# Router stage of a graph network: a buffer for every tile of neighbour rows, gates of edge-free nodes by place, a fixed order on PE

## The chip, the cores and the metric

The kernel runs on one core of one Trainium2 chip. Its time is the device time in microseconds (us) of one execution; with one core there is no other to wait for. The core has separate engines that run side by side, each with its own queue of instructions: PE (TensorE, matmuls; PEld is its weight loads), DVE (VectorE), ACT (ScalarE), POOL (GpSimd) and SP (SyncE, which here only starts transfers). They wait for each other through semaphores. [...] an *indirect* transfer takes one row of a table for each of the 128 partitions, by a column of indices, and here POOL starts all of these.

## The reference

A graph network of two layers over 3125 nodes with 256 features. The change concerns the last part, a mixture of four experts whose router looks at a node's neighbours. Cut to what matters:

```python
def _forward(x, edge_index, W_gat, att_src, att_dst, b_gat, ln_gamma, ln_beta, W1, b1, W2, b2):
    h = (x_flat @ W_gat).reshape(M, HEADS, NUM_EXPERTS)          # 4 heads x 4 experts
    loops = jnp.arange(M)                                         # every node is its own neighbour too
    src = concatenate([edge_index[0], loops]); dst = concatenate([edge_index[1], loops])
    e = leaky_relu((h * att_src).sum(-1)[src] + (h * att_dst).sum(-1)[dst], 0.2)
    ee = exp(e - segment_max(e, dst)[dst])
    alpha = ee / (segment_sum(ee, dst)[dst] + 1e-16)
    agg = segment_sum(h[src] * alpha[:, :, None], dst).reshape(M, 16) + b_gat
    scores = _layernorm(agg, ln_gamma, ln_beta).reshape(M, HEADS, NUM_EXPERTS).mean(1)
    topk_s, topk_i = top_k(scores, 2)
    w = softmax(topk_s, axis=-1)
    for ei in range(NUM_EXPERTS):
        g = where(topk_i == ei, w, 0.0).sum(-1)
        hh = gelu(x @ W1[ei] + b1[ei])
        out = out + g[..., None] * (hh @ W2[ei] + b2[ei])
```

A node without incoming edges has only itself as a neighbour, so its `alpha` is 1 and its `agg` is its own `h` plus the bias.

## The kernel before

The nodes lie in 25 tiles of 128 (`NT`). The layers before the router keep them in one order ("places"); the result rows `xs` of that order stay in SBUF. For the router's attention the nodes are sorted anew by their number of edges: in this second order 16 tiles are *busy* and need 36, 23, 21, ... 10 neighbour slots (`SLOTS2`, 279 in all), and 9 tiles are *free*, without edges.

The layer code has a helper `router_rows` that is called in six parts. For up to five tiles it normalizes the rows, stores them transposed to DRAM (`normed`, on SP), makes `h` (16 values) and the source attention (4 values) per node as `hx`, and scatters these 20 values by node number into a DRAM table `htab` (on POOL).

`routed_by_slots` is the router stage. It starts at about 2536 us and runs to the end.

- **Gathers.** L2107 fetches the 20 values of each node of the second order from `htab`, 25 gathers, free tiles first. `neighbours(t)` (L2137) fetches one row per neighbour slot into a tile `ed` with one gather for every slot (L2140). The tiles `ed` share three buffers: `more(3)` starts three tiles' gathers before the main loop, and `more(1)` the next after each `attend`.
- **Attention and gates.** `attend` (L2145) adds the two attention terms, takes leaky relu and maximum on DVE, the exp on ACT (L2156), and sums up the weighted rows on DVE (L2158). `gates` (L2168) takes up to five tiles: bias, layernorm (sqrt on ACT, L2194), mean over heads, the two best of four, their softmax (exp on ACT, L2215). At its end it makes, tile by tile, a 0/1 matrix `los` on DVE (L2228, three buffers) and a matmul (L2229) that adds the gates into a PSUM tile `placed` at the nodes' places. `own` (L2161) stands in for `attend` for the free tiles. `step` (L2244) does one busy tile, or five free ones, as a whole: it writes DVE, ACT and PE work in one go.
- **Experts.** The main loop takes four tiles at a time (the last time one), loads their transposed rows `xT` (L2330), and for each pair of experts calls `hidden` twice and later `outs`. `hidden` (L2261): 16 matmuls into four PSUM tiles `ph` (L2267, three buffers) and four gelus on ACT (L2269). `outs` (L2272): for each tile a bias matmul (L2276) and 8 matmuls (L2279) into a PSUM tile `po` (three buffers). Each float32 matmul is two passes on PE, and so two records in the profile. The outputs of the first 20 tiles (`NF`) are copied to `f` in SBUF by ACT (L2282), since the gates are not known yet. From the 21st tile on, all steps that are left are run, `gate` is copied out of `placed` (L2287), and the outputs are added to `xs` straight from PSUM (`add`, L2298).
- **Kept tiles.** With each tile of the last five, two of the 20 kept tiles are finished too, once for each pair of experts: `kept` does four `add`s from `f` on DVE. `put` scatters a finished tile to the output (L2303, POOL).
- **Order.** For ACT and DVE the program order is the order on the engine (`manual_schedule`). PE, POOL and SP are ordered by a scheduler. The main loop keeps a `clock`, 2.4 us per tile for a `hidden` and 4.6 us per tile for a pair of `outs`; before each `hidden` it runs the steps whose estimated gather time (1.25 us a slot) plus 8 lies before that clock.

Of the kernel before, what the change touches and what calls it, by code (L numbers as in the profile page):

```python
# [12 lines left out]
F32 = mybir.dt.float32  # L13
BF16 = mybir.dt.bfloat16
I32 = mybir.dt.int32
AF = mybir.ActivationFunctionType
# [5 lines left out]
P = 128  # L22
N = 3125
D = 256
# [872 lines left out]
class Fast(Net):  # L897
# [955 lines left out]
    def layers(self):  # L1853
# [7 lines left out]
        with ExitStack() as octx:  # L1861
# [40 lines left out]
            with tc.tile_pool(name="l1_edge", bufs=2, reuse_waits="tile") as ep, \  # L1902
# [93 lines left out]

                def router_rows(ts):
# [12 lines left out]
                    for i, t in enumerate(ts):  # L2010
# [11 lines left out]
                                            axis=AX.X, op=OP.add)  # L2022
                    for i, t in enumerate(ts):
                        ins = nc.gpsimd.indirect_dma_start(
                            out=self.htab[:NP, :], in_=hx[:, i, :], in_offset=None,
                            out_offset=bass.IndirectOffsetOnAxis(ap=self.pid[:, t:t + 1], axis=0)).ins

                        if t:
                            tc.declare_no_dep(ins, group="htab", reason="other nodes")
                        tc.add_to_no_dep_group("htab", ins)  # L2030
# [59 lines left out]
    def routed_by_slots(self):  # L2090
# [6 lines left out]
        free = [t for t in range(NT) if not SLOTS2[t]]  # L2097
        busy = [t for t in range(NT) if SLOTS2[t]]
        with ExitStack() as ctx:
# [4 lines left out]
                engines={mybir.EngineType.Activation, mybir.EngineType.DVE}))  # L2104
            hx = keep.tile([P, NT, 24], F32, name="hx")
            for t in free + busy:
                nc.gpsimd.indirect_dma_start(  # L2107
                    out=hx[:, t, :20], out_offset=None, in_=self.htab[:, :],
                    in_offset=bass.IndirectOffsetOnAxis(ap=self.pid2[:, t:t + 1], axis=0))
# [12 lines left out]
            for j, n in enumerate(("gat_asrc", "gat_adst", "gat_b", "gat_gamma", "gat_beta")):  # L2122
# [4 lines left out]
            his = keep.tile([P, NT, NT], F32, name="his")  # L2127
            nc.vector.tensor_tensor(his, self.iota[:, None, :NT].to_broadcast([P, NT, NT]),
                                    self.place2[:, 0].unsqueeze(2).to_broadcast([P, NT, NT]), op=OP.is_equal)
            placed = ps.tile([P, NT, NE], F32, name="placed")  # L2130
            f = keep.tile([P, NF, NE, D], F32, name="f")
# [4 lines left out]
            def neighbours(t):  # L2136
                S = SLOTS2[t]  # L2137
                ed = work.tile([P, max(SLOTS2) + 1, 20], F32, name="ed", bufs=3)
                for s in range(S):
                    nc.gpsimd.indirect_dma_start(  # L2140
                        out=ed[:, s, :], out_offset=None, in_=self.htab[:, :],
                        in_offset=bass.IndirectOffsetOnAxis(ap=self.nbrs[t][:, s:s + 1], axis=0))
                return ed

            def attend(t, ed, agg):  # L2145
# [9 lines left out]
                nc.vector.tensor_sub(e, e, m.to_broadcast([P, S + 1, 4]))  # L2155
                nc.scalar.activation(e, e, AF.Exp)  # L2156
# [4 lines left out]
            def own(ts):  # L2161

                agg = work.tile([P, 5, 20], F32, name="agg")
                nc.vector.tensor_copy(agg[:, :len(ts), :16], hx[:, ts[0]:ts[-1] + 1, :16])
                nc.vector.memset(agg[:, :, 16:], 1.0)
                return agg

            def gates(ts, agg):  # L2168

                n = len(ts)  # L2170
                t0 = ts[0]
# [11 lines left out]
                s = work.tile([P, 5, 8], F32, name="s")[:, :n]  # L2183
# [7 lines left out]
                tmp = work.tile([P, 5, 16], F32, name="tmp")[:, :n]  # L2191
                nc.vector.tensor_mul(tmp, f16, f16)
                nc.vector.tensor_reduce(s[:, :, 1], tmp, axis=AX.X, op=OP.add)
                nc.scalar.activation(s[:, :, 2], s[:, :, 1], AF.Sqrt, bias=self.eps[:, 0:1], scale=1.0 / 16)  # L2194
# [4 lines left out]
                sco = work.tile([P, 5, NE], F32, name="sco")[:, :n]  # L2199
# [3 lines left out]
                pick = work.tile([P, 2, 5, NE], F32, name="pick")  # L2203
                for j in range(2):
# [7 lines left out]
                    if j == 0:  # L2212
                        nc.vector.scalar_tensor_tensor(sco, o, -BIG, sco, op0=OP.mult, op1=OP.add)
                nc.vector.tensor_sub(s[:, :, 5], s[:, :, 5], s[:, :, 4])
                nc.scalar.activation(s[:, :, 5], s[:, :, 5], AF.Exp)  # L2215
# [5 lines left out]
                nc.vector.tensor_add(pick[:, 0, :n], pick[:, 0, :n], pick[:, 1, :n])  # L2221

                what = work.tile([P, 5, NT, NE], F32, name="what", bufs=1)
                nc.vector.tensor_mul(what[:, :n], his[:, t0:t0 + n].unsqueeze(3).to_broadcast([P, n, NT, NE]),
                                     pick[:, 0, :n].unsqueeze(2).to_broadcast([P, n, NT, NE]))
                for i, t in enumerate(ts):
                    los = work.tile([P, P], F32, name="los", bufs=3)
                    nc.vector.tensor_scalar(los, self.iota, self.place2[:, 1, t:t + 1], None, op0=OP.is_equal)  # L2228
                    nc.tensor.matmul(placed, los, what[:, i], start=(t == order[0]), stop=(t == order[-1]))  # L2229


            order = free + busy
            steps = []
            now = 1.25 * NT + 4
            for i in range(0, len(free), 5):
                steps.append((now, free[i:i + 5], None))
# [7 lines left out]
            def more(ahead):  # L2244

                for t in busy[len(eds):len(eds) + ahead]:
                    eds[t] = neighbours(t)

            def step():
                _, ts, t = steps.pop(0)  # L2250
                if t is None:
                    gates(ts, own(ts))
                    return
                if ts[0] not in aggs:
                    aggs[ts[0]] = work.tile([P, 5, 20], F32, name="agg")
                attend(t, eds[t], aggs[ts[0]][:, t - ts[0], :])
                more(1)
                if t == ts[-1]:
                    gates(ts, aggs[ts[0]])
# [12 lines left out]
            def outs(ts, hs, e0):  # L2272

                for j, t in enumerate(ts):
                    po = ps.tile([P, 2, D], F32, name="po", bufs=3)
# [8 lines left out]
                    if steps or len(done) == 0:  # L2284
                        while steps:
                            step()
                        nc.vector.tensor_copy(gate, placed)  # L2287
                        done.append(True)
# [4 lines left out]
                    for _ in range(2):  # L2293
                        if late:
                            kept(late.pop(0))
# [15 lines left out]
            def kept(t):  # L2311
                for e in range(NE):
                    add(t, e, f[:, t, e, :])
                put(t)

            done = []
            puts = []
            late = list(range(NF))

            tmp = work.tile([P, NT, 16], F32, name="what", bufs=1)  # L2320
            nc.vector.tensor_mul(tmp, hx[:, :, :16], att[:, 1:2, :].to_broadcast([P, NT, 16]))
            nc.vector.tensor_reduce(hx[:, :, 20:], tmp.rearrange("p t (h e) -> p t h e", e=4), axis=AX.X, op=OP.add)
            more(3)
            clock = 0.0
            last = None
            for t0 in range(0, NT, 4):
# [4 lines left out]
                for e0 in (0, 2):  # L2331
                    hs = []
                    for e in (e0, e0 + 1):
                        while steps and steps[0][0] + 8 < clock:
                            step()
                        hs.append(hidden(ts, xT, e))
                        clock += 2.4 * w
                        if e == e0 and last:
                            outs(*last)
                            last = None  # L2340
                    clock += 4.6 * w
                    last = ts, hs, e0
# [90 lines left out]
```

## Time and profile before

| | us |
|---|---|
| three runs | 3212.45, 3179.78, 3209.07 |
| their median | 3209.07 |
| the profiled execution | 3207.38 |
| its span | 3205.6 |
| busy in the span: PE | 1915.6 |
| PEld | 1173.4 |
| DVE | 1484.3 |
| ACT | 787.2 |
| POOL | 1580.0 |

The span runs from the first to the last instruction that the profiler recorded on this core. 1.8 us of the execution lie around it. The router's stretch, 2540 to 3206 us, has these rows (instruction group, partitions x elements, count, then busy us and mean ns of one, then idle time of the engine just before them and what ended it):

```profile
L2107 POOL DMA_INDIRECT hx<-htab,pid x25 | 23.7, 949 | 12.2 <-issue 7.3 <-DMA htab<-hx,pid 4.9
L2267 PE MATMUL ph<-xT,w 128*128 128x512 f32 x384 | 197.5, 664 | 64.7 <-ACT h L2269 38.3 <-issue 17.0 <-DMA xT<-normed 9.3
L2269 ACT ACTIVATE h<-ph,b 128x512 f32<-128x512 f32 x96 | 63.5, 687 | 215.6 <-PE ph L2267 116.9 <-remote 70.0 <-PE po L2279 15.0
L2282 ACT COPY f<-po 128x512 f32<-128x512 f32 x40 | 22.5, 588 | 210.9 <-remote 140.7 <-PE po L2279 66.0 <-PE po L2276 4.1
L2298 DVE SCALAR_TENSOR_TENSOR xs<-f,gate,xs 128x256 f32<-128x256 f32 x80 | 37.8, 483 | 2.1
L2303 POOL DMA_INDIRECT out<-xs,pid x25 | 25.1, 1003 | 56.7 <-DVE xs L2298 55.3 <-issue 1.5
```

"issue" means that the engine waited for nothing that the profile shows; "remote" that the releaser was not made out. The profile also gives the span in 40 equal slices of 80 us, with the busy share of each engine in tenths and the clock that TensorE was granted (`PEclk`, tenths of full speed), and can cut any stretch into windows with each engine's busy time and number of instructions.

### The profile page before, as it was taken

What the parts mean: (1) busy time and instruction counts of PE and PEld (TensorE: products, weight loads), DVE (VectorE), ACT (ScalarE), POOL (GpSimd) and SP (SyncE); (2) the same over time, 40 slices, a digit from 0 to 9 for tenths busy, and PEclk for the clock granted to TensorE, in tenths of its full rate; (3) what the DMA queues carried; (4) which work ended last, traced back from release to release, by engine and by line L of the source; (5) the groups of instructions that cost most, each with busy time, mean ns of one, the idle gap of its engine ahead of it and who ended that gap; (6) DMA issues with size and microseconds to landing.
All of it is one profiled execution on the core that took longest, in us unless ns stands there. A gap on an engine that the chain in (4) does not pass through costs nothing. (4 is left out here: it accounts for less than half of the span.)

```text
span 3205.6 us, 25047 instructions
## 1 busy us (share of the span) xinstructions
PE 1915.6 (60%) x7318; PEld 1173.4 (37%) x7318; DVE 1484.3 (46%) x4053; ACT 787.2 (25%) x2273; POOL 1580.0 (49%) x1675
## 2 busy tenths in 40 slices
PE   0166754567566768777726364755556534866678
PEld 0133432234333434443414243534334312533346
DVE  6366556544444545310436565866657301111027
ACT  1022221111111212111205242434344301322122
POOL 3555446746535453446165664546551272445443
PEclk9887876778778889888857676767666666978789
DMA  4522223222212221100064464546451200000001
GB/s 129 161 75 76 60 82 100 79 63 83 74 47 78 67 74 53 34 14 20 32 195 140 138 178 130 150 131 177 141 156 53 77 9 10 12 6 13 12 7 42
DMA packets 121376, 254.52 MB, mean 79 GB/s; under 512 B 36594, under 2 KB 61926, under 8 KB 120972
## 3 DMA queue, kind: packets, MB, share of 16 engines
q0 software_dynamic: 82656, 196.67, 21.7%
q1 hardware_dynamic: 31688, 49.09, 4.6%
q10 hardware_dynamic: 6884, 7.04, 0.7%
q8 instruction: 61, 1.00, 0.1%
q14 instruction: 87, 0.71, 0.1%
HBM read 228.93 MB, written 23.76 MB: 79 GB/s over the span
## 5 line engine op out<-in xcount | busy, mean ns | idle before, releaser
L1384 POOL DMA_INDIRECT g<-xtab,src x444 | 441.9, 995 | 413.4 <-DVE ed L1287 134.6
L1929 POOL DMA_INDIRECT kv<-kvtab,src x444 | 430.0, 968 | 317.4 <-issue 113.4
L2140 POOL DMA_INDIRECT ed<-htab,nb x279 | 264.7, 949 | 281.3 <-issue 184.0
L1966 ACT ACTIVATE kv<-kv,sc 128x64 f32<-128x64 f32 x1196 | 293.2, 334 | 52.9 <-issue 31.9
L1240 POOL DMA_INDIRECT gl<-gsrc,sidx x256 | 251.7, 983 | 79.1 <-issue 77.7
L1968 PE MATMUL pu<-kv,ident 128*128 128x256 f32 x888 | 270.1, 449 | 17.5 <-ACT kv L1966 12.1
L2279 PE MATMUL po<-w,h 128*128 128x256 f32 x800 | 210.5, 406 | 89.5 <-issue 88.8
L2267 PE MATMUL ph<-xT,w 128*128 128x512 f32 (+1 forms) x448 | 205.2, 609 | 64.7 <-ACT h L2269 38.3
L1706 PE MATMUL ph<-xT,w 128*128 128x512 f32 (+1 forms) x448 | 237.4, 660 | 0.0
L1723 PE MATMUL po<-w,h 128*128 128x256 f32 x800 | 218.0, 417 | 11.1 <-ACT h L1709 10.1
L1968 PEld LDWEIGHTS pu<-kv,ident 128*128 128x128 f32 x888 | 184.4, 223 | 67.2 <-ACT kv L1966 32.2
L1391 DVE SCALAR_TENSOR_TENSOR acc<-g,wt,acc 128x256 f32<-128x256 f32 x419 | 202.9, 484 | 12.2 <-DVE acc L1391 0.2
L2279 PEld LDWEIGHTS po<-w,h 128*128 128x128 f32 x800 | 156.8, 200 | 141.2 <-issue 123.6
L1935 DVE TENSOR_TENSOR kv<-kv,pr 128x1024 f32<-128x1024 f32 (+3 forms) x121 | 132.8, 1124 | 109.2 <-remote 70.4
L1723 PEld LDWEIGHTS po<-w,h 128*128 128x128 f32 x800 | 157.3, 207 | 48.6 <-issue 18.5
L1709 ACT ACTIVATE h<-ph,b 128x512 f32<-128x512 f32 (+1 forms) x112 | 71.7, 641 | 383.0 <-PE ph L1707 168.9
L1354 PE MATMUL pT<-typT,sel 18*128 18x128 bf16 (+9 forms) x229 | 32.9, 275 | 197.3 <-DVE typT L1345 145.1
L2267 PEld LDWEIGHTS ph<-xT,w 128*128 128x128 f32 x448 | 87.4, 210 | 165.8 <-issue 117.2
L1368 PE MATMUL pr<-self.relb,ohT 128*128 128x128 bf16 x687 | 82.7, 276 | 105.1 <-issue 57.6
L2158 DVE TENSOR_TENSOR ed<-ed 128x288 f32<-128x288 f32 (+12 forms) x16 | 7.5, 466 | 285.5 <-ACT ed L2156 285.5
L1756 POOL DMA_INDIRECT kvtab<-kv,pid x25 | 24.3, 972 | 224.6 <-DVE kv L1750 139.2
L1937 DVE TENSOR_TENSOR kv<-kv,q 128x1024 f32<-128x1024 f32 (+3 forms) x121 | 132.4, 1123 | 0.0
(443 smaller groups left out, 3197.3 us busy)
## 6 DMA issues: line engine op xcount, KB each, us to landing
dr<-in_gat_dst_row SPq DMA_DIRECT2D x32, 512.0 KB
g<-xtab,src POOLq DMA_INDIRECT x444
kv<-kvtab,src POOLq DMA_INDIRECT x444
own<-xq SPq DMA_DIRECT2D x25, 256.0 KB
xq<-own SPq DMA_DIRECT2D x25, 256.0 KB
ed<-htab,nb POOLq DMA_INDIRECT x279
w<-in_ex_w ACTq DMA_DIRECT2D x2, 2048.0 KB
gl<-gsrc,sidx POOLq DMA_INDIRECT x256
```

The costliest lines, as they stand in the source:

```text
L1240: ins = nc.gpsimd.indirect_dma_start(out=self.gl[:, :], out_offset=bass.IndirectOffsetOnAxis(ap=self.sidx2[:, c:c + 1], axis=0), in_=self. ...
L1384: self.moved = nc.gpsimd.indirect_dma_start(out=g[:, s % 4, :], out_offset=None, in_=self.xtab[:, :], in_offset=bass.IndirectOffsetOnAxis( ...
L1391: nc.vector.scalar_tensor_tensor(acc, g[:, s % 4, :], self.wts[t][:, s:s + 1], acc, op0=OP.mult, op1=OP.add)
L1706: nc.tensor.matmul(ph[:, :n], w1[:, k, mc], xT[:, k, :n], start=(k == 0), stop=False)
L1723: nc.tensor.matmul(pos[j // 2][:, j % 2], this[:, j * P:(j + 1) * P], w2[:, m, :], start=False, stop=(m == M - 1 and (j % 2 == 1 or j == w ...
L1929: nc.gpsimd.indirect_dma_start(out=kv[:, j, :], out_offset=None, in_=kvtab[:, :], in_offset=bass.IndirectOffsetOnAxis(ap=self.srcs[t][:, g ...
L1935: nc.vector.tensor_tensor(k4, k4, rr[:, r0:r0 + n].unsqueeze(2).to_broadcast([P, n, 4, HD]), op=OP.add)
L1966: nc.scalar.activation(v[:, h * HD:(h + 1) * HD], v[:, h * HD:(h + 1) * HD], AF.Copy, scale=sc[:, s, h:h + 1])
L1968: nc.tensor.matmul(pu, self.ident, v, start=(s == 0), stop=(s == SLOTS[t] - 1))
L2140: nc.gpsimd.indirect_dma_start(out=ed[:, s, :], out_offset=None, in_=self.htab[:, :], in_offset=bass.IndirectOffsetOnAxis(ap=self.nbrs[t][ ...
L2267: nc.tensor.matmul(ph[:, :w], w1[:, e, k, m * P:(m + 1) * P], xT[:, :len(ts), k, :], start=(k == 0), stop=(k == KB - 1))
L2279: nc.tensor.matmul(po[:, i], hs[i][:, m, j * P:(j + 1) * P], w2[:, e0 + i, m, :], start=False, stop=(i == 1 and m == M - 1))
```

## The change

1. `router_rows` also stores `hx` to a new DRAM tile `hown`, in the order of places (six stores on SP).
2. PE is added to `manual_schedule`: the program order is now PE's order too.
3. `hx` is gathered for the 16 busy tiles only. `ed` has a buffer of its own for every tile, and `neighbours` is called for all 16 tiles before the main loop.
4. Nodes without edges: `gates` is run once over all 25 tiles at the start of the stage, on `hown` (one load on SP), with the result in place order; it goes without `los` and `placed`. Once `placed` is complete, nodes whose sum of gates there is under 0.25 take the gates of this pass.
5. `attend`, `gates` and the new `to_places` are generators. They yield before an exp, a sqrt and the `placed` matmuls, and `go_on` takes every open one a stage further before each `hidden`.
6. `los` has four buffers instead of three, `po` four instead of three; `f` is allocated after the pass over 25 tiles, in its space.
7. `weighed`: eight of the 20 kept tiles are weighted on PE. For each expert ACT makes a diagonal matrix of the gates, and a matmul adds the weighted `f` into a PSUM tile; DVE adds that once.

```diff
...
+                self.hown = self.dram.tile([P, NT, 20], F32, name="hown")
...
                                             axis=AX.X, op=OP.add)
+                    nc.sync.dma_start(self.hown[:, t0:t0 + n, :], hx[:, :n, :])
...
-                engines={mybir.EngineType.Activation, mybir.EngineType.DVE}))
-            hx = keep.tile([P, NT, 24], F32, name="hx")
-            for t in free + busy:
+                engines={mybir.EngineType.Activation, mybir.EngineType.DVE, mybir.EngineType.PE}))
+            nb = len(busy)
+            hx = keep.tile([P, nb, 24], F32, name="hx")
+            for t in busy:
                 nc.gpsimd.indirect_dma_start(
...
-            f = keep.tile([P, NF, NE, D], F32, name="f")
...
-                ed = work.tile([P, max(SLOTS2) + 1, 20], F32, name="ed", bufs=3)
+                ed = keep.tile([P, S + 1, 20], F32, name=f"ed{t}")
...
+                yield
                 nc.scalar.activation(e, e, AF.Exp)
...
-            def own(ts):
-
-                agg = work.tile([P, 5, 20], F32, name="agg")
-                nc.vector.tensor_copy(agg[:, :len(ts), :16], hx[:, ts[0]:ts[-1] + 1, :16])
-                nc.vector.memset(agg[:, :, 16:], 1.0)
-                return agg
-
-            def gates(ts, agg):
-
-                n = len(ts)
-                t0 = ts[0]
+            def gates(n, agg, pool, most, out):
...
+                out.append(pick[:, 0, :n])
+
+            def to_places(ts, g):
+
+                n, t0 = len(ts), ts[0]
+                what = work.tile([P, 4, NT, NE], F32, name="what", bufs=1)
...
+                loss = []
+                for t in ts:
+                    loss.append(work.tile([P, P], F32, name="los", bufs=4))
+                    nc.vector.tensor_scalar(loss[-1], self.iota, self.place2[:, 1, t:t + 1], None, op0=OP.is_equal)
+                yield
                 for i, t in enumerate(ts):
-                    los = work.tile([P, P], F32, name="los", bufs=3)
-                    nc.vector.tensor_scalar(los, self.iota, self.place2[:, 1, t:t + 1], None, op0=OP.is_equal)
-                    nc.tensor.matmul(placed, los, what[:, i], start=(t == order[0]), stop=(t == order[-1]))
-
-
-            order = free + busy
+                    nc.tensor.matmul(placed, loss[i], what[:, i], start=(t == busy[0]), stop=(t == busy[-1]))
+
+
             steps = []
-            now = 1.25 * NT + 4
-            for i in range(0, len(free), 5):
-                steps.append((now, free[i:i + 5], None))
+            now = 1.25 * len(busy) + 4
...
+            under = []
+
+            def go_on(clock=None):
+
+                while True:
+                    for u in list(under):
+                        if next(u, under) is under:
+                            under.remove(u)
+                    while steps and (clock is None or steps[0][0] + 8 < clock):
+                        _, ts, t = steps.pop(0)
+                        under.append(step(ts, t))
+                        next(under[-1])
+                        if clock is None:
+                            break
+                    if clock is not None or not (under or steps):
+                        return
...
-                    po = ps.tile([P, 2, D], F32, name="po", bufs=3)
+                    po = ps.tile([P, 2, D], F32, name="po", bufs=4)
...
-                    if steps or len(done) == 0:
-                        while steps:
-                            step()
+                    if len(done) == 0:
+                        go_on()
+
+                        none = work.tile([P, NT], F32, name="none", bufs=1)
                         nc.vector.tensor_copy(gate, placed)
+                        nc.vector.tensor_reduce(none, gate, axis=AX.X, op=OP.add)
+                        nc.vector.tensor_scalar(none, none, 0.25, None, op0=OP.is_lt)
+                        nc.vector.tensor_mul(own[0], own[0], none.unsqueeze(2).to_broadcast([P, NT, NE]))
+                        nc.vector.tensor_add(gate, gate, own[0])
                         done.append(True)
...
-                    for _ in range(2):
+                    for i in range(2):
                         if late:
-                            kept(late.pop(0))
+                            (weighed if i and t % 5 < 4 else kept)(late.pop(0))
...
+            def weighed(t):
+
+                po = ps.tile([P, D], F32, name="po", bufs=4)
+                for e in range(NE):
+                    dg = work.tile([P, P], F32, name="los", bufs=4)
+                    nc.scalar.activation(dg, self.ident, AF.Copy, scale=gate[:, t, e:e + 1])
+                    nc.tensor.matmul(po, dg, f[:, t, e, :], start=(e == 0), stop=(e == NE - 1))
+                nc.vector.tensor_add(self.xs[:, t, :], self.xs[:, t, :], po)
+                put(t)
...
+            for t in busy:
+                eds[t] = neighbours(t)
+
+            own = []
+            with tc.tile_pool(name="rt_own", bufs=1, reuse_waits="tile") as once:
+                agg = once.tile([P, NT, 20], F32, name="agg")
+                nc.sync.dma_start(agg, self.hown[:, :, :])
+                nc.vector.memset(agg[:, :, 16:], 1.0)
+                for _ in gates(NT, agg, once, NT, own):
+                    pass
+                kept_own = keep.tile([P, NT, NE], F32, name="own")
+                nc.vector.tensor_copy(kept_own, own[0])
+                own[0] = kept_own
+            late_f = ctx.enter_context(tc.tile_pool(name="rt_f", bufs=1, reuse_waits="tile"))
+            f = late_f.tile([P, NF, NE, D], F32, name="f")
...
-            more(3)
...
-                        while steps and steps[0][0] + 8 < clock:
-                            step()
+                        go_on(clock)
...
```

## Prediction

> **What bounds the kernel now.** I read the tenths of the span first, then the costliest groups, then the waits of the router's stretch alone (2540 to 3206 us, the only part that the change touches apart from six small stores), and then that stretch cut into windows at the starts and ends of the bursts of neighbour gathers.
>
> ```profile
> PE   0166754567566768777726364755556534866678
> POOL 3555446746535453446165664546551272445443
> PEclk9887876778778889888857676767666666978789
> ...
> L2140 POOL DMA_INDIRECT ed<-htab,nb x279 | 264.7, 949 | 281.3 <-issue 184.0
> L2279 PE MATMUL po<-w,h 128*128 128x256 f32 x800 | 210.5, 406 | 89.5 <-issue 88.8
> ```
>
> The router is the last eight slices. PE is half idle where POOL is at 7, and fuller where POOL is lower. The idle time ahead of L2279 is put down to "issue": PE waited for nothing that the profile shows. The waits of the stretch (waiting, waited for: us in total, times, longest):
>
> ```profile
> PEld po L2279 <- issue: 123.6, 115, 3.3
> POOL ed L2140 <- ACT h L2269: 96.1, 3, 74.9
> ```
>
> 115 waits of at most 3.3 us are not waits for data. The windows (start:end, length, then busy us and count of PE, PEld, DVE, ACT, POOL, the granted clock, DMA share, GB/s):
>
> ```profile
> 2556.00:2690.00 134.00, 49.75 (x93) 21.96 (x91) 3.64 (x13) 9.94 (x14) 89.24 (x95) 0.59 0.08 7
> 2695.00:2749.00 54.00, 47.80 (x150) 27.85 (x149) 18.53 (x81) 23.14 (x32) 0.20 (x1) 0.94 0.03 10
> 2942.00:2955.00 13.00, 13.00 (x57) 9.64 (x56) 9.47 (x43) 6.47 (x9) 9.52 (x11) 1.00 0.08 9
> 2955.00:2985.00 30.00, 1.19 (x5) 0.36 (x4) 0.20 (x2) 0.00 (x0) 18.87 (x20) 0.57 0.07 7
> 2985.00:3004.00 19.00, 18.86 (x49) 10.00 (x50) 2.56 (x10) 7.01 (x11) 0.00 (x0) 0.86 0.09 28
> ```
>
> In the first, POOL issues gathers without a gap (the burst is 2542.8 to 2673.0, 105 of them, one per 1.25 us) and PE finishes 93 matmuls in 134 us; in the second POOL has nothing and PE does 150 in 54 us. The last three show one burst (30 gathers, 2942.4 to 2978.7): for its first 13 us PE is full, then almost nothing until some 6 us after its end, then full again. The timeline inside the first burst (start us, us, engine line operation, idle before):
>
> ```profile
> 2642.54 0.58 PE L2279 MATMUL po<-w,h 128*128 128x256 f32 x1 [2.21 <-issue]
> 2642.93 0.95 POOL L2140 DMA_INDIRECT ed<-htab,nb  x1 [0.30 <-issue]
> 2643.94 0.29 PEld L2279 LDWEIGHTS po<-w,h 128*128 128x128 f32 x1 [2.50 <-issue]
> 2644.19 0.95 POOL L2140 DMA_INDIRECT ed<-htab,nb  x1 [0.30 <-issue]
> 2645.34 0.58 PE L2279 MATMUL po<-w,h 128*128 128x256 f32 x1 [2.22 <-issue]
> ```
>
> A load, a matmul, a load, a matmul, each 1.40 us after the other: PE crawls at one instruction per 1.40 us. All seven bursts of 20 or more do so: it begins 11 to 16 us after a burst's start and ends 3 to 17 us after its last gather, later the longer the burst, close to the burst's start plus 1.40 us per gather (105: 2542.8 + 147 = 2690; 30: 2942.4 + 42 = 2984). The burst of 17 slows PE for some 8 us only. Earlier stages show it too, with other tables and rows. What couples the two engines no view shows; I use it as measured.
>
> It accounts for the stage. PE's work at full pace is 24 hidden calls of 16 matmuls x 0.434 = 6.95, four of one tile at 1.95, 50 outs at 3.96 and the placed matmuls 6: 379 us. PE works from 2552 to 3195.5, 643 us. The 264 us between is the sum of the crawls, about 115 + 17 + 32 + 8 + 28 + 29 + 22 + 23 = 274.
>
> **The change part by part.** The profiled execution took 3207.4 us, 1.8 more than its span, and 1.7 less than the median 3209.1 (two runs lie within 3.5 us of it, one 29 below).
>
> *Own buffers for the neighbour rows.* The instruction order of the changed kernel has 16 hx gathers and all 279 ed gathers in a row on POOL, each waiting only for the gather eight back, and no buffer. POOL's gaps (96 us behind the gelu at L2269, others behind exps) are gone, and with them the windows in which PE ran at full pace. One burst of 304 - 9 = 295 from 2543 ends at 2543 + 295 x 1.252 = 2912. By the measured law the crawl runs from 2556 to 2543 + 295 x 1.40 = 2956. In it PE gets 400 / 1.40 = 286 instructions, 143 matmuls; at the stage's mean of 379 / 1348 = 0.28 us that is 40 us of work, and 5 us were done before. If PE is instead let go with the last gather (2912 + 5), the end is 40 us earlier.
>
> *PE's own work.* 9 placed matmuls less (-1 us). weighed: 8 tiles x 4 matmuls x 2 passes x 0.216 = +14 us. In all 379 - 1 + 14 = 392; 45 done by 2956, 347 left: PE ends at 2956 + 347 = 3303.
>
> *The end.* From PE's last matmul to the last scatter is 10 us now. On DVE, weighed takes away 8 x 4 adds at 0.48 and puts in 8 adds from PSUM, -11 us, beside PE, so nothing while PE leads and a few us at best in the last tiles. ACT gains 32 diagonals of 128x128 (nearest row: 334 ns for 128x64), say 0.4 x 32 = 13 us, beside PE too; each feeds a matmul directly, so in fixed PE order a late one holds the hidden and outs matmuls behind it. I put 3 us for that, up to 13 if nothing covers it.
>
> *Gates by place.* One pass over 25 tiles at the program's start: about 12 wide operations at 0.58 us (the nearest row, L2321, 128x400) and 22 narrow at 0.25, 15 us with the sqrt and exp, each with a table load of 1.28, ahead of the first gelu on ACT. PE has three ph buffers and then waits, to about 2567; but at 1.40 us an instruction it loses only some 2 us of work (8 to 20 if PE were at pace). The two free-tile passes that go had stood beside PE. The five small DVE operations at the gate: 1.5 us, and the first f copy waits for the space of the pass, long over.
>
> *Fixed PE order and steps.* placed matmuls may wait for an attend (now 28.9 us at most, at the crawls' ends). Gathers come at 1.25 us and PE is behind them throughout, so the rows are there: 0, and up to 20 us if an estimate of the clock puts a gate before its exp.
>
> *The rest.* hx: 9 gathers fewer, -11 us of POOL, counted in the 295. hown: six stores on SP, which wait for DVE's reduce and stand before the next xq load there; a small SP load costs 0.43 us to issue, xq has three buffers: 0 to 2 us, I take 1. agg load, 256 KB before the xT load on SP: 1 us. po 4 buffers: a gain only where PE waits for an f copy (0.7 us): 0.
>
> Sum: PE's end 3303, + 5 for stalls, + 10: span 3318, + 1.8: **3320**, 113 over the profiled run.
>
> *A rule against it.* The row: 13 us of full PE in a burst, then 1.19 us busy in 30. The Trainium skill, page "Perfetto Trace Analysis", section "Optimization Strategy", reads consistent bubbles otherwise: there may not be enough SBUF or PSUM for the next tile's buffers. POOL's 96 us behind one gelu fit that, and by the rule own buffers are the cure: gathers end at 2912, the last attend and gates about 18 us later, then the last outs and kept work, 56 + 14 us as now: a span of 3000. By the row the bubbles in POOL are the time in which PE works, and the sum is 3320. I go with the row, because all seven bursts show it.
>
> **The rivals.** *B: the price is per gather, however they are grouped.* 274 us over 304 gathers is 0.90 each; 9 fewer save 8, the additions cost 14 + 7: 3207 - 8 + 21 = 3220. For it: little, as short bursts do fall under the price (17 gathers lost 8 us, 105 lost 115). A partial crawl that lets go midway belongs here: 3080 to 3260.
>
> *C, the other side: the crawl does not hold in the long burst, and the gathers' chain is the bound.* What matters is whether PE's pace inside the burst is near 0.28 us a matmul; then PE's 392 us are beside the gathers from 2552 to about 2944, and the end is 3000 to 3005, 205 us faster. It decides when PE does more than 153 us of its work before 2956, instead of 45: then the 239 left end before 3195, where PE ends now. For it: POOL is held by buffers 281 us, and these are truly removed. Against it: the 134 us window, where nothing ended the crawl before the burst did.
>
> *D: the change does not do what it says.* If the gathers still came in groups (SBUF short), nothing would be gained, 3207 to 3225; the order shows them in a row, so this is inside B's chance.
>
> **How the numbers follow.** A (the crawl for the whole burst) 0.76, own range 3275 to 3345 (release right at the burst's end; all stalls uncovered). B 0.08, half of it faster, most of the rest within 1%. C 0.16. About 1% (32 us) is what a measurement of this kernel can tell from no change. Faster 0.16 + 0.04 = 0.20, the same 0.03, slower 0.76 + 0.01 = 0.77. The range 3130 to 3350 leaves out C and the ends, a little under 0.2.
>
> **What would show it.** Right: one POOL burst from 2543 to about 2912 without a gap; inside it PE at 2.8 us a matmul, about 20 to 25 matmuls in any 65 us, PEclk 0.57 to 0.60; full pace from about 2956 and 340 us of it; first gelu near 2567; the POOL wait behind L2269 gone. Wrong: PE busy above nine tenths while POOL gathers, or a PE that comes back inside the burst; then C or B. If the burst is as said but PE's full pace begins before 2912, the law of the release is wrong.

## The result, and the profile after

The changed kernel took 3281.3 us (median of four executions, 3266.5 to 3289.7), the kernel before 3204.6 us (four executions, 3179.8 to 3212.5). The medians alone give 1.024 times as long; the ratio on record is 1.027, interval 1.023 to 1.032. The profiled execution took 3266.5 us, its span 3264.6.

The page of the changed kernel: tenths of the span in 40 slices, then two groups (busy us, mean ns | idle before, releaser).

```profile
PE   0276755466667777686435556555564322159998
POOL 3555456565455453543456656555413777720003
PEclk9887867688778889898666767666676655569998
...
L2142 POOL DMA_INDIRECT ed<-htab,nb x279 | 279.2, 1001 | 86.2 <-issue 85.9
L2288 PE MATMUL po<-w,h 128*128 128x256 f32 x800 | 211.0, 405 | 127.0 <-issue 126.7
```

POOL's gathers are now one block (four slices at 7 and one at 2). PE sinks to 3, 2, 2 and 1 under the first four, and stands at 9 once POOL has nothing to do. POOL's idle time before the gathers fell from 281 to 86 us, and PE's "issue" time at L2288 rose from 89 to 127 us. The waits of the router's stretch (waiting, waited for: us in total, times, longest):

```profile
PEld po L2288 <- issue: 156.4, 110, 3.3
POOL ed L2142 <- issue: 81.0, 262, 0.9
PE placed L2231 <- DVE los L2228: 4.5, 1, 4.5
```

POOL waits for no buffer any more: its longest wait is 0.9 us. Three windows of the same profile (start:end, length, busy us and count of PE, PEld, DVE, ACT, POOL, granted clock, DMA share, GB/s):

```profile
2600.00:2860.00 260.00, 53.33 (x72) 20.45 (x72) 0.00 (x0) 6.47 (x10) 199.33 (x197) 0.51 0.10 10
...
2884.00:2910.00 26.00, 6.46 (x12) 2.97 (x11) 0.00 (x0) 0.69 (x1) 0.85 (x1) 0.50 0.01 1
...
2910.00:3265.00 355.00, 335.88 (x1206) 217.93 (x1206) 102.44 (x340) 139.93 (x219) 24.84 (x25) 0.97 0.04 15
```

PE has 72 matmul records in the 260 us beside the gathers, 12 in the 26 us after the last gather, and 1206 in the 355 us from there to the end. The records are an uneven count of its pace: among the 72 is a gap of 65.6 us, for which the profile names no wait. What PE delivers is even, as the copies of `f` on ACT show (start us, us, engine line operation, idle before):

```profile
2705.66 0.59 ACT L2291 COPY f<-po 128x512 f32<-128x512 f32 x1 [46.97 <-remote]
2753.26 0.59 ACT L2291 COPY f<-po 128x512 f32<-128x512 f32 x1 [47.01 <-issue]
```

Each copy needs 17 matmul records and as many loads. The copies start 47.6 us apart, which is 34 x 1.40. The second of these and the next one, at 2800.9 us, fall inside the gap of the records, which runs from 2747 to 2813 us.

The clearest measure is the router's own length, from the first hx gather to the end of the span: 662.8 us before, 766.0 after, so 103 more. The kernel before was profiled once only, so 662.8 is the measure for all runs below. The executions come to that first gather at different times, although nearly the same instructions stand ahead of it: 2542.8 us before, 2498.6 here, 2553.2 when the changed kernel was profiled again. The medians therefore differ by less (77 us) than the router does.

### The profile page after: what moved, and what is told of

Read it like the earlier page. It is cut to its first block, busy times and chain, and to the rows that moved or that the text cites. A ratio compares the mean times of both kernels' runs of the same rounds, so it can differ in the third digit from the quotient of the medians.

```text
span 3264.6 us, 25096 instructions
## 1 busy us (share of the span) xinstructions
PE 1927.5 (59%) x7364; PEld 1176.3 (36%) x7364; DVE 1467.4 (45%) x3987; ACT 798.0 (24%) x2302; POOL 1587.4 (49%) x1666
## 5 line engine op out<-in xcount | busy, mean ns | idle before, releaser
L2142 POOL DMA_INDIRECT ed<-htab,nb x279 | 279.2, 1001 | 86.2 <-issue 85.9
L2288 PE MATMUL po<-w,h 128*128 128x256 f32 x800 | 211.0, 405 | 127.0 <-issue 126.7
L2288 PEld LDWEIGHTS po<-w,h 128*128 128x128 f32 x800 | 155.9, 200 | 173.7 <-issue 156.4
L2317 POOL DMA_INDIRECT out<-xs,pid x25 | 24.8, 993 | 351.1 <-DVE xs L2312 341.5
L2276 PEld LDWEIGHTS ph<-xT,w 128*128 128x128 f32 x448 | 86.6, 208 | 285.8 <-issue 253.4
```

The lines of the kernel that those rows point to most:

```text
L2142: nc.gpsimd.indirect_dma_start(out=ed[:, s, :], out_offset=None, in_=self.htab[:, :], in_offset=bass.IndirectOffsetOnAxis(ap=self.nbrs[t][ ...
L2276: nc.tensor.matmul(ph[:, :w], w1[:, e, k, m * P:(m + 1) * P], xT[:, :len(ts), k, :], start=(k == 0), stop=(k == KB - 1))
L2288: nc.tensor.matmul(po[:, i], hs[i][:, m, j * P:(j + 1) * P], w2[:, e0 + i, m, :], start=False, stop=(i == 1 and m == M - 1))
```

## The experiments

Every comparison below is with the kernel before on the same chip at the same time. The chips turned out to differ, and this is the main finding: on three of those below the kernel before took 3188 to 3215 us (medians), on two 2491.

**A bench of PE beside gathers.** Each phase does this, with its own number of gathers `n`, memset `width`, partitions and columns:

```python
for i in range(200):
    nc.tensor.matmul(po, w, x, start=(i == 0), stop=(i == 199))
for j in range(max(n, 40)):
    if j < n:
        nc.gpsimd.indirect_dma_start(out=got[:parts, j, :cols], ...)
    if width:
        nc.gpsimd.memset(fill[:, :width], 0.0)
```

> A bench of its own (its output is zeros; nothing of the network is computed): ten phases, each with 200 dense matmuls of 128x256 float32 on PE (400 passes, about 87 us at 0.216 us a pass) beside 40 indirect gathers of 128 rows on POOL, one after the other; the phases differ in what stands between the gathers (nothing, POOL memsets of 1, 128, 256, 512 columns), in the partitions of a gather (128, 96, 64), in the row (80 B, 1 KB), one has plain loads from POOL's queue and one has no transfer. Theory (something serves a gather of 128 rows in 1.40 us and PE falls behind it once gathers come faster than that, every 1.25 us): without a gap PE is at full pace for 11 to 16 us, then at 1.40 us an instruction until 40 x 1.40 = 56 us after the start, and does about 60 + 30 passes by then; with gathers 1.45 us apart or more (128 columns and up) it never crawls, and PE's 400 passes take about 87 us; 96 and 64 rows need 1.05 and 0.70 us, so they never make it crawl. Rival (any gather in flight beside PE slows it, each costs 0.9 us): all phases with 40 gathers lose about 36 us, whatever the gap. Second rival (the crawl comes from something of the router itself, its semaphores or waits): no phase here loses anything.

Measured: nothing slows PE in any phase; all take 87 to 89 us (the first phase 89.2, the others 86.6). But the kernel before took 2491 us on this chip. The window over the 40 back-to-back gathers of the first phase (PE, PEld, DVE, POOL):

```profile
13.00:63.00 50.00, 50.00 (x224) 43.63 (x223) 0.00 (x0) 37.73 (x40) 1.00 0.12 9
```

So on this chip the theory failed on the bench as a whole, and the second rival seemed right. The bench was run again, where the kernel before took 3215 us:

> The bench of the first run once more. Where the kernel before takes about 2490 us: ten phases of 87 us, no crawl, as before. Where it takes about 3200 us, as the first bench's theory said: the phase with back-to-back gathers crawls (PE let go at 56 us), the phases with 128 and more columns of memset do not, nor do the gathers of 96 and 64 rows; rival: all phases with gathers lose about 36 us.

```profile
13.00:33.00 20.00, 20.00 (x85) 17.23 (x84) 0.00 (x0) 15.05 (x16) 1.00 0.10 9
33.00:67.00 34.00, 8.38 (x19) 4.25 (x17) 0.22 (x1) 23.02 (x25) 0.57 0.10 8
67.00:134.00 67.00, 66.19 (x298) 57.43 (x297) 0.00 (x0) 0.00 (x0) 0.96 0.00 0
383.00:439.00 56.00, 55.26 (x252) 47.24 (x250) 0.00 (x0) 49.55 (x79) 1.00 0.10 8
474.00:538.00 64.00, 64.00 (x298) 56.34 (x297) 0.00 (x0) 57.53 (x79) 1.00 0.09 7
...
702.00:740.00 38.00, 9.83 (x25) 5.32 (x23) 0.22 (x1) 24.45 (x28) 0.56 0.06 4
934.00:955.00 21.00, 21.00 (x98) 18.49 (x99) 0.00 (x0) 20.94 (x40) 1.00 0.18 19
```

Lines one to three are the first phase: PE full for 20 us, 19 passes in 34 us, full again from 67 us, which is 13.4 (the first gather) + 40 x 1.35. The crawl is here without anything of the router. Line four has 256 columns of memset after each gather, one gather per 1.445 us, and PE nearly at full pace (the phase took 89.1 us); line five 512 columns, 1.66 us, and no loss (86.6); with 1 and 128 columns (1.355 and 1.339 us) the phases took 124 and 119 us. Line six has 64 partitions instead of 128, and crawls like the first; so do 96 partitions and rows of 1 KB (122 to 123 us). Line seven has 40 plain loads from POOL's queue, one per 0.53 us, and no crawl; but they are over in 21 us, and the crawl of the first phase began only after 20. So it is the pace of indirect gathers that counts on this bench, with a limit between 1.36 and 1.45 us, and not their rows or bytes: the expectation for 96 and 64 partitions was wrong, and so was 128 columns, whose memset of 0.22 us moved the gathers by 0.09 us only.

The two traces of this bench differ in one more thing. The rows of the gathers' transfers, without the crawl and with it (count, then median us from issue to landing):

```profile
got<-tab,nx POOLq DMA_INDIRECT x280, 2.4
```

```profile
got<-tab,nx POOLq DMA_INDIRECT x280
```

The second row has no landing time, because most of the semaphore updates by which transfers report their end are missing from that trace. Counted in the traces, the first phase has 640 of them without the crawl, 16 per gather, and 145 with it. On the chip with the crawl, the six phases that crawl have 113 to 175, the one at 1.445 us has 291, and those at 1.66 us and with plain loads have all 640. The router shows the same: 488 records from the first neighbour gather to 10 us after the last in the changed kernel, 4561 where own buffers do no harm (the next run), and 4322 in the kernel paced twice (below). So records go missing where PE crawls. Whether one causes the other is open, and so is whether the recording has a part in the crawl: each execution timed here has a recorded span and clock, and no run shows PE without the recording.

**The own buffers alone.** The kernel before, with

```diff
-                ed = work.tile([P, max(SLOTS2) + 1, 20], F32, name="ed", bufs=3)
+                ed = keep.tile([P, S + 1, 20], F32, name=f"ed{t}")
...
-            more(3)
+            more(len(busy))
...
-                more(1)
```

and, for room, `his` in bfloat16 and two buffers for `los`.

> The kernel before with one part of the change alone: every tile of neighbour rows in its own buffer, all 279 gathers in a row before the main loop (to make room the 0/1 table his is bfloat16 and los has two buffers instead of three). Theory (one burst makes PE crawl to its end): 304 gathers end at 2543 + 380 = 2923, PE is let go by 2968, then 379 - 45 = 334 us of PE and 10 of tail: about 3312 in the frame of the first profile, 3300 to 3325. Rival (the fixed PE order, the steps or the weighing make the loss, not the buffers): 3190 to 3215. Second rival (own buffers help, as the gaps of POOL behind the gelus go): below 3180.

Measured where the kernel before took 2491 us: 2490.0 us, ratio 0.9995 (0.9975 to 1.0014). None of the three cases had thought of a chip without the crawl. Again on another chip:

> The kernel before with own buffers for the neighbour rows alone. Where the kernel before takes about 3200 us: theory (the single burst is all of the loss, about 140 us between three buffers and own ones in the changed kernel) 3300 to 3345; rival (own buffers cost this only together with the fixed PE order, which keeps PE from taking other work) 3190 to 3230. Where it takes about 2490 us: no change again.

Measured: 3295.2 us against 3187.7, ratio 1.032 (1.024 to 1.039); the router's length is 764.0 us against 662.8. The windows show the same two halves as the changed kernel:

```profile
2600.00:2900.00 300.00, 53.04 (x95) 24.14 (x95) 6.09 (x28) 8.77 (x12) 229.78 (x229) 0.51 0.11 8
2946.00:3297.00 351.00, 332.78 (x1183) 211.19 (x1183) 116.21 (x367) 126.97 (x189) 25.01 (x25) 0.97 0.05 16
```

Own buffers alone make the whole loss (101 of 103 us), in PE's old order too.

**The own buffers undone.** The changed kernel, with

```diff
-                ed = keep.tile([P, S + 1, 20], F32, name=f"ed{t}")
+                ed = work.tile([P, max(SLOTS2) + 1, 20], F32, name="ed", bufs=3)
...
-            for t in busy:
-                eds[t] = neighbours(t)
+            more(3)
...
                 yield from attend(t, eds[t], agg[:, t - ts[0], :])
+                more(1)
```

> The changed kernel with that part alone undone: three buffers for the neighbour rows, the first three tiles gathered ahead, the next after each attend. Theory (the single burst is the whole loss; the other parts cost about 12 us): 3210 to 3235. Rival (the loss lies in the PE order, the steps or the weighing): 3265 to 3290, as the changed kernel.

Measured where the kernel before took 2491 us: 2500.9, ratio 1.0036 (1.0016 to 1.0056). Its window there shows what PE does without the crawl:

```profile
2060.00:2200.00 140.00, 140.00 (x467) 85.05 (x465) 13.97 (x37) 48.52 (x70) 106.15 (x112) 1.00 0.15 16
```

112 gathers in 140 us, one after the other, and PE not idle for a moment. POOL ran all 279 neighbour gathers in one row with three buffers only (2049.9 to 2398.9 us): where PE is on time, so are the gelus, the attends and the buffers. The same kernel on a chip with the crawl, below, has POOL wait 100.8 us for gelus, so POOL's 96 us behind gelus in the kernel before are a consequence of the crawl.

> The changed kernel with three buffers for the neighbour rows. Where PE crawls: theory (the single burst is the loss) 3210 to 3235 where the kernel before takes 3205 and the changed one 3281; rival (the PE order, the steps or the weighing) 3265 to 3290. Where it does not: 1.0036 as in the last run.

Measured where the kernel before took 3215 us: 3179.5, ratio 0.989 (0.983 to 0.995); the router's length is 636.7 us, against 766.0 of the changed kernel on the same chip. So the own buffers cost 129 us here, and the rest of the change, expected at +12, *gains*: 26 us by the router's length against the profile of the kernel before, which is of another chip, and 35 by the medians on this one.

**The changed kernel again**, unedited, on that same chip:

> The changed kernel as it is, beside the kernel before on the same chip. In the last runs PE did not crawl at all (the kernel before took 2491 us there, not 3205), so the first question is whether the crawl belongs to the chip. If the kernel before takes about 3200 us here, the crawl is back, and the changed kernel should again be 1.02 to 1.03 times as long. If it takes about 2490 us, there is no crawl, and the theory (the loss was the crawl alone) expects 0.998 to 1.004: PE full beside one burst, the burst the same length in both. Rival (the change costs something of its own as well): over 1.01 without a crawl too.

Measured: 3320.4 us against 3214.6, ratio 1.0335 (1.027 to 1.040), a little over what was expected. The router's length is 766.0 us, the same as in the first profile to a tenth.

**The weighing left out.** `kept(late.pop(0))` for all 20 tiles, in the changed kernel and in the one with three buffers.

> The changed kernel with all 20 kept tiles added on DVE, none weighted on PE. Theory (the weighing costs 64 passes of PE, 14 us, in a stretch where PE is the bound, and its DVE gain is hidden): 10 to 14 us less than the changed kernel. Rival (DVE is the bound of the last tiles, the weighing gains): 5 to 15 us more.

> The changed kernel with three buffers for the neighbour rows and without the weighing on PE, to tell what the other parts of the change do beside the own buffers: with three buffers and the weighing the ratio was 0.989, where 1.004 had been expected (+12 us). Theory (the weighing's 64 passes of PE are on the path, 14 us, less some 3 us of DVE): 0.984 to 0.987. Rival (the weighing is what gained, as DVE's adds hold the last tiles): 0.992 to 1.0. Where the kernel before takes about 2490 us: 0.996 to 1.0.

Measured: without the crawl (changed kernel, no weighing) 2486.4 us against 2491.2, ratio 0.9988 (0.9973 to 1.0002); the changed kernel itself was not run on that chip, so the weighing can only be estimated there: three buffers with the weighing took 2500.9 us, own buffers without it 2486.4, and own buffers alone were worth nothing, which leaves some 14 us for it. With the crawl (three buffers, no weighing) 3140.6 against 3195.9, ratio 0.984 (0.977 to 0.990; the kernel before spreads from 3148.1 to 3199.5 there), and a router of 614.8 us against 636.7 with the weighing, on two different chips. The intervals of the two ratios overlap; the router's lengths, of one execution each, put the weighing at 22 us. So it lies at 14 to 22. The profile of the kernel with three buffers and weighing has, for the weighing's matmuls:

```profile
L2342 PE MATMUL po<-f,los 128*128 128x256 f32 x64 | 17.0, 413 | 1.9 <-ACT los L2341 1.9
```

What gained, then, is another part. One row of the waits moved much. Before, and with three buffers:

```profile
PE placed L2229 <- DVE los L2228: 57.6, 3, 28.9
```

```profile
PE placed L2231 <- DVE los L2228: 4.4, 1, 4.4
```

In the kernel before the placed matmuls stand where PE has to wait for their `los`; in the fixed order with steps, which yields between `los` and matmul, that wait is 4.4 us. It fell into the crawls in part, so its 53 us are not all gain. No run changed the order alone, and so this share is read from the waits and not shown by an experiment.

**The gathers paced.** The changed kernel with a POOL memset after each neighbour gather, and 1.5 instead of 1.25 us a slot in the estimate of the steps:

```diff
                 for s in range(S):
-                    nc.gpsimd.indirect_dma_start(
+                    tc.keep_in_program_order(nc.gpsimd.indirect_dma_start(
                         out=ed[:, s, :], out_offset=None, in_=self.htab[:, :],
-                        in_offset=bass.IndirectOffsetOnAxis(ap=self.nbrs[t][:, s:s + 1], axis=0))
+                        in_offset=bass.IndirectOffsetOnAxis(ap=self.nbrs[t][:, s:s + 1], axis=0)))
+                    tc.keep_in_program_order(nc.gpsimd.memset(pause, 0.0))
...
-                    now += 1.25 * SLOTS2[t]
+                    now += 1.5 * SLOTS2[t]
```

> The changed kernel with a POOL memset of 128x128 after every neighbour gather (0.22 us on the bench, so a gather every 1.47 us), and 1.5 us instead of 1.25 a slot in the estimate of the steps. Where PE crawls: if the crawl needs gathers faster than one per 1.40 us, PE is at full pace, gathers end at 2500 + 295 x 1.47 = 2934, PE has 80 us left then: 3030 to 3060, 150 us below the kernel before. If each gather has its price, 3280 to 3310. Where PE does not crawl: the gathers' chain is 279 x 0.22 = 61 us longer and is what the last tiles wait for: 50 to 61 us more than the kernel before.

Measured: 3285.5 us against 3214.6, ratio 1.024 (1.015 to 1.033), a router of 745.6 us. That is in the range of a price per gather, but the spacing to be tested was not reached: the gathers stood 1.34 us apart, under the limit of the bench. PE crawled to 2965 us, close to the burst's start plus 1.40 us per gather (2961), though at about twice the pace of the changed kernel:

```profile
2650.00:2800.00 150.00, 59.62 (x104) 25.25 (x104) 0.00 (x0) 7.84 (x12) 124.26 (x215) 0.58 0.11 11
```

104 matmuls in 150 us, and gelus mostly 5.6 us apart, which is eight instructions at 0.70 us. So the crawl weakens as the gathers come nearer to the limit. One memset of 320 columns does not fit: `f` needs 80 KB per partition of the on-chip memory SBUF, and the wider `pause` leaves 79.25. With the memset of 128 columns written twice:

> The changed kernel with two POOL memsets of 128x128 after every neighbour gather (one gave a gather every 1.34 us in the router and on the bench, and the crawl stayed; a second adds about 0.2): a gather every 1.55 us. Where the kernel before takes about 3200 us: if spacing over 1.40 us alone ends the crawl, PE is full beside the gathers, these end at 2550 + 16 x 1.27 + 279 x 1.55 = 3003, some 88 us are left then, as on the chip without the crawl: 3070 to 3105, 3 to 4 % below the kernel before. If the router's gathers make PE crawl at any spacing: 3290 to 3330. Where it takes about 2490 us: 279 x 0.3 = 84 us more than the kernel before.

Measured: 3084.2 us against 3195.9, ratio 0.967 (0.961 to 0.973), the best of all on such a chip, and 2.0% under the shortest of the kernel before there, 3148.1; the router takes 561.5 us, 204 less than the changed kernel. The gathers are 1.586 us apart. The groups of POOL, and two windows:

```profile
L2144 POOL DMA_INDIRECT ed<-htab,nb x279 | 265.9, 953 | 48.5 <-issue 48.5
L2147 POOL MEMSET pause<- 128x128 f32 x279 | 62.0, 222 | 0.1
L2148 POOL MEMSET pause<- 128x128 f32 x279 | 57.1, 205 | 16.1
```

```profile
2550.00:2760.00 210.00, 207.19 (x697) 126.62 (x697) 22.14 (x73) 71.42 (x103) 179.49 (x391) 0.99 0.12 15
2760.00:2920.00 160.00, 112.91 (x353) 65.87 (x351) 26.18 (x96) 45.53 (x65) 137.11 (x301) 0.85 0.10 11
```

PE is full for the first 210 us beside the gathers: 697 matmuls, where the changed kernel did 72 in 260 us. In the second window PE waits, but for data: the order of steps counted on 1.5 us a gather, and the gathers came every 1.586.

```profile
PE placed L2235 <- DVE los L2232: 74.8, 2, 41.2
```

The last kernel was to mend this, with the second memset cut to 16 columns and no weighing:

> A version that may beat both: own buffers, the second memset after a gather cut to 16 columns (about 0.1 us less, a gather every 1.48 us instead of 1.586, and so within the 1.5 us a slot that the order of the steps counts on), and no tile weighted on PE. Where the kernel before takes about 3200 us: if 1.48 us is still over the limit, 279 x 0.1 = 29 us and some 12 us for the weighing less than with two memsets: 3035 to 3055, a ratio of 0.950 to 0.957. If 1.48 is under the limit in the router, the crawl is back: over 1.0. Where it takes about 2490 us: 279 x 0.23 - 12 = 50 us more than the kernel before.

It met a chip without the crawl: 2553.3 us against 2491.2, ratio 1.026 (1.023 to 1.028), where +50 us had been expected and +62 was measured. Pacing is a loss where PE does not crawl. What this version is worth where PE does, no run shows.

## Why the prediction was right, and where not

- **The bound and the mechanism.** Right on chips of the first kind. One burst, one crawl: it ended at 2910 us, 25 us after the last gather's end, and 2498.6 + 295 x 1.40 is 2911.6. In the repeated profile PE is let go at about 2966, and 2553.2 + 413 is also 2966. The first gelu starts 25.5 us after the first gather (24 expected). From the end of the crawl to the end of the span it took 354.6 us (347 + 5 + 10 = 362 expected). The whole router: 775 us expected, 766.0 measured, twice. Two of the signs were not met as written: PE's records show 18 matmuls in one stretch of 113 us, where 35 to 43 were to stand, though ACT's copies show the pace of 1.40 us throughout; and the granted clock was 0.50 to 0.51, not 0.57 to 0.60.
- **The time.** 3320 was forecast for one execution at the frame of the first profile, and 3281 is the median. The 9 us of the router's length are the smaller part. The larger is the stretch ahead of the router: this execution came 44 us earlier to its first gather than the profiled one before, the repeated one 10 us later. The sum took the start from one profile as fixed; over eight profiles on chips that crawl it lies between 2498.6 and 2566.9 us. That the changed kernel took 3320.4 us in the repeat, the forecast to the microsecond, is luck: its router was 9 us shorter than in the sum and began 10 us later.
- **The own buffers.** The sum's law for 304 gathers gives 2543 + 426 = 2969, and 334 + 10 us of work behind it, a router of 770 us; own buffers alone measured 764.0.
- **The terms beside it.** Beside own buffers they came out: the whole change has a router of 766.0 us and own buffers alone 764.0, so the rest is +2, where 775 - 770 = 5 was expected. Beside three buffers they do not. The weighing stood at 14 us and lies at 14 to 22. "Fixed PE order and steps" stood at 0 to +20, and a gain is likely to lie there: with three buffers the whole rest of the change is 26 us shorter than the kernel before, 48 without the weighing. The row that points to it, PE waiting 57.6 us for `los`, was in the waits that the prediction drew on, but was put to the crawls' ends.
- **The gathers' own pace.** The burst was to last 369 us and took 385 (1.306 us a gather; 1.25 in the short bursts). It changes nothing, since the crawl's end goes by 1.40.
- **Rival B** (a price per gather) falls with the bench: 40 gathers 1.445 us apart cost 2.5 us, 40 at 1.66 nothing, 40 at 1.25 cost 33 to 36. **Rival C** (no crawl in a long burst) is wrong where there is a crawl. Where there is none, it is wrong as well: the kernel before does not have the loss then either, and own buffers alone are at 0.9995. The Trainium skill's rule on consistent bubbles (page "Perfetto Trace Analysis", section "Optimization Strategy"), by which the prediction had worked out a span of 3000 us against the 3264.6 measured, speaks of gaps on the engine that should be saturated. That engine is PE here, and the gaps that fitted the rule were POOL's, a consequence of PE's.
- **What the prediction did not see:** that the crawl could be a matter of the chip. It was right about a change on a chip that crawls. On the other kind every variant without added memsets that was run there lay within 0.5% of the kernel before; the changed kernel itself was not.

What makes the chips differ stays open. The gathers have the same pace, packets and bytes on both, and no view shows what PE waits for; what differs beside PE is how many landings the traces hold. Each chip was met once, so it isn't shown either that it is the chip, and not its condition at that time.

## What to carry to other kernels

When an engine is slow with nothing to wait for, lay its windows over what the other engines do before you give one of these more freedom: a buffer that holds a queue back may be all that keeps another engine at pace. Here removing the wait cost about 3%, and spacing out the same queue gained about 3%. Run the kernel before on more than one chip before you tune against such a slowness, since a milder form of the cure cost 2.6% where it does not exist.

## What the runs showed of the hardware

- The same program takes 3200 us on some chips and 2491 us on others, with medians that agree within 1% on each kind. The difference is PE's crawl, in the earlier stages too: the first hx gather comes at 2499 to 2567 us with it, at 2029 to 2033 us without.
- While it crawls beside gathers 1.25 us apart, PE takes one instruction, load or matmul, per 1.40 us (about one per 0.70 us beside gathers 1.34 us apart), until the burst's start plus 1.35 to 1.40 us per gather. It comes with indirect gathers that POOL issues less than about 1.4 us apart for longer than 11 to 20 us, whatever their partitions (64 to 128) and rows (80 B to 1 KB). Gathers 1.445 us apart cost 2.5 us in 89, those 1.586 and 1.66 us apart and 21 us of plain loads every 0.53 us cost nothing.
- On the chips where PE crawls the traces lack most semaphore updates of the gathers' transfers in the crawl (145 of 640 in the bench's first phase); without the crawl all are there.
- The granted clock falls to 0.50 to 0.58 in the crawl. That cannot make it: a pass of 0.22 us would be 0.44 if it took twice as long at 0.50, and not 2.8.
- POOL's memset of 128x128 takes 0.22 us, but one after each gather moved the gathers from 1.25 to 1.34 us apart; a second one to 1.586.
